# One-hots copied by ScalarE ahead of each gather's three products, in a graph network of two layers on one core

## The chip, the cores and the metric

The kernel runs on 1 core of one Trainium2 chip. The metric is device time in microseconds (us) of one execution, as the median of 10 executions. The core has five engines that run side by side and wait for each other by semaphores: TensorE (PE in the profile; its weight loads have a row of their own, PEld), VectorE (DVE), ScalarE (ACT), GpSimd (POOL) and SyncE (SP). An engine's instructions run in the order in which they stand in its queue.

## The reference

x is 12500 nodes of 256 features, and there are 200000 edges, sorted by target (dst). Cut to what matters:

```python
def _gcn_conv(x, W, b, src, dst, n):
    h = x @ W
    deg = jax.ops.segment_sum(ones, dst, num_segments=n)
    dinv = jnp.where(deg > 0, jax.lax.rsqrt(deg), 0.0)
    msgs = h[src] * (dinv[src] * dinv[dst])[:, None]
    return jax.ops.segment_sum(msgs, dst, num_segments=n) + b

def _L0(h):                       # edges plus one loop per node
    h = h @ W_pre + b_pre
    h = relu(_gcn_conv(h, W1, b1, src, dst, n))
    h = relu(_gcn_conv(h, W2, b2, src, dst, n))
    return h @ W_post + b_post

x = x + _L0(relu(layernorm(x)))
x = x + _L1(relu(layernorm(x)))   # attention over 4 heads of one edge per node
```

The weight is in the two convolutions: 200000 rows of a table are gathered by source, and summed by target.

## The kernel before

A first stage reads the edges, counts degrees, normalises x and writes a table of scaled rows to memory. Then `convolve` (L1155) runs twice, and a last stage does the attention layer.

**How a convolution is tiled.** The 200000 edges are cut into 112 chunks (`NCH`) of 14 gathers (`J`), a gather being 128 edges, whose source rows one indirect DMA fetches, one to a partition. The sorted targets of a chunk lie within a window of 128 nodes. So the sum by target is a matrix product: for each gather a one-hot matrix of 128 edges by 128 targets is the stationary operand (it has to be loaded as weights), and the gathered rows are the moving one, and all of the chunk is accumulated in one PSUM tile, `facc`.

**Three parts.** A float32 row is split into three bfloat16 rows whose sum it is (`to_parts`, L1475), and from chunk `SINCE` on in the first convolution, and throughout the second, the gather fetches the three side by side from the table `parts`. Then `many` is 3, and L1411 issues three products with the same one-hot and three different moving operands, into the same `facc`. Before `SINCE` the table is float32 and there is one product. Each product has its own load of weights in TensorE's queue.

**Buffers.** Nine gathers (`ONE`) share one `fgot` tile; the second convolution has four such tiles and the first five. GpSimd may run ahead of TensorE by what they hold, and then waits until TensorE is done with a tile. One VectorE instruction makes the one-hots of a whole chunk (`one_hots`, L1246, called by `hot_of` at L1410 when j is 2, for the chunk after), into `fhot`, which has three buffers of 14 one-hots each.

**Order of the work.** The loop at L1382 runs over the gathers (t counts them) and writes the instructions in the order wanted, with no scheduler behind it. For each gather: the indirect DMA on GpSimd (L1402); perhaps the one-hots of the next chunk; the products on TensorE (L1411); and then `run(t)`, which writes what is due at t. Due work is put down by `close` (L1290) at a chunk's end: ScalarE copies `facc` to `fsums` at once (L1293), 8 gathers later TensorE turns the sums (`turn_sums`, L1205), 13 later VectorE adds them into a sliding buffer, and where a tile of 128 nodes is then complete, `shift` (L1316) puts down the steps of `finish1` or `finish2`, each so many gathers later:

- `finish1` (L1446), first convolution: +6 TensorE's product with the folded weights (L1453) and the two-row product for the bias (L1454); +10 three ScalarE passes (L1458, L1460, L1462) and a DMA issued from ScalarE's queue (L1463); +12 VectorE's split into parts and SP's write of them (L1476 to L1479).
- `finish2` (L1542), second convolution: +6 TensorE (L1550); +8 VectorE and ScalarE (L1557, L1560); +12 TensorE (L1566); +14 VectorE, and a root on ScalarE (L1571 to L1579); +16 ScalarE (L1587); +26 TensorE (L1592); +28 ScalarE (L1596); +32 TensorE (L1605); +34 a ScalarE copy and two DMAs issued from its queue (L1613 to L1616).

There are 98 such tiles of nodes in 112 chunks. Every engine meets its instructions in the order in which the loop wrote them, so what ScalarE has to do for the steps stands between what it does for the gathers. L1663 is a tile that is never used and only keeps addresses apart. The last stage (from L1702) has, at L1749 and L1751, products that ScalarE copies out of PSUM by turns.

Of the kernel before, what the change touches and what calls it, by code (L numbers as in the profile page):

```python
# [8 lines left out]
F32 = mybir.dt.float32  # L9
BF16 = mybir.dt.bfloat16  # L10
I32 = mybir.dt.int32
AF = mybir.ActivationFunctionType
# [5 lines left out]
P = 128  # L18
# [395 lines left out]
def fast_path(  # L414
# [26 lines left out]
    nc = tc.nc  # L441
# [4 lines left out]
    J = 14  # L446
# [17 lines left out]
    nj = [min(J, -(-(E - c * CE) // P)) for c in range(NCH)]  # L464
# [115 lines left out]
    def raw_scaled(c):  # L580

        k = slice(c * J, (c + 1) * J)
        nc.vector.reciprocal(raw_sc[:, k], raw_sc[:, k])
        nc.vector.tensor_mul(raw_sc[:, k], raw_sc[:, k], d_src[:, k])
        nc.vector.scalar_tensor_tensor(raw_mv[:, k, 0], raw_mv[:, k, 0], -1.0, raw_sc[:, k],
                                       op0=ALU.mult, op1=ALU.mult)
        nc.vector.tensor_copy(raw[c][:, :, D], d_src[:, k])
        for j in range(J):
            v = raw[c][:, j, :D]
            i = c * J + j  # L590
            nc.scalar.activation(v, v, AF.Relu, bias=raw_mv[:, i, 0:1], scale=raw_sc[:, i:i + 1])
# [563 lines left out]
    def convolve(ep, table, stride, width, ahead, with_sum, psum, prepare, finish, parts, since,  # L1155
# [64 lines left out]
        def begin_sums():  # L1220
            for n0, rows in first_rows:
                v, n = {}, min(P, BW - n0)
                new_turned(v)
                turn_sums(rows, 0, v)
                nc.vector.tensor_copy(state["buf"][0][:, :, n0:n0 + n], v["pt"][:, :KC, :n])
                if with_sum:
                    nc.vector.tensor_copy(state["buf"][1][:, n0:n0 + n], v["ps"][:, 0, :n])
# [18 lines left out]
        def one_hots(h, to):  # L1246
            n = to.shape[1]
            nc.vector.tensor_tensor(h, iota_p[:, None, :].to_broadcast([P, n, P]),  # L1248
                                    to[:, :, None].to_broadcast([P, n, P]), ALU.is_equal)

        def new_hot(c):
            if since == 0:
                return ep.tile([P, J, P], BF16, name="fhot", bufs=3)
            h = ep.tile([P, J, P], F32, name="fhot", bufs=3)
            if c < since:
                return h
            h = h.rearrange("p j n -> p (j n)").bitcast(BF16)[:, :J * P]
            return h.rearrange("p (j n) -> p j n", n=P)

        def hot_of(c):  # L1260

            n = nj[c]
            h = new_hot(c)
            one_hots(h[:, :n, :], to_0 if lacking and c == 0 else to_t[:, c, :n])
            return h

        def new_rows_of():
            if with_sum:
                return new_got()
            return rows_p.tile([P, ONE, 3 * stride], BF16, name="fgot", bufs=ahead)  # L1270

        def late_sums():

            h = new_hot(0)
            one_hots(h, to_t[:, 0, :])
            froms = new_rows_of().rearrange("p j d -> p (j d)")[:, :J * D]
            froms = froms.rearrange("p (j d) -> p j d", d=D)
            assert stride == TW * P and D == TW * P
            for i in range(TW):
                one_hots(froms[:, :, i * P:(i + 1) * P], from_0[:, i, :])  # L1280
            px = psum.tile([P, KC, P], F32, name="fpt", bufs=1)
            for i in range(TW):
                for j in range(J):
                    nc.tensor.matmul(px[:, i, :], froms[:, j, i * P:(i + 1) * P], h[:, j, :],
                                     start=(j == 0), stop=(j == J - 1))
            many = work.tile([P, KC, P], F32, name="fz", bufs=2)
            nc.scalar.activation(many, px, AF.Copy)
            return many, [load_rows((NT - TW + i) * P, P) for i in range(TW)]
# [70 lines left out]
        hots = {0: hot_of(0)}  # L1359
        raw_lohi, raw_m = {}, {}  # L1360
        for c in range(1, len(raw)):
            raw_lohi[c] = raw_ends(c, rows_p.tile([P, 2 * CE], BF16, name="lohi_t",
                                                  bufs=len(raw) - 1))
# [4 lines left out]
        def raw_ahead(c, j):  # L1368
# [8 lines left out]
            elif j + 1 == J:  # L1377
                raw_sum(c, raw_m[c], fpt())()
                raw_scaled(c)

        assert KC == TW
        for t, (c, j) in enumerate(tiles):  # L1382
            if j == 0:
                acc = psum.tile([P, width], F32, name="facc", bufs=2 if not with_sum else 3)

            many = 1 if c < since else 3
            if many == 1:
                if j == 0:
                    gots = (raw + [spare])[c] if raw and c <= len(raw) else new_rows_of()
                got = gots[:, j, :]  # L1390
            else:
                i = (t - since * J) % ONE
                if i == 0:
                    gots = new_rows_of()
                    if since:
                        gots = gots.rearrange("p j d -> p (j d)").bitcast(BF16)
                        gots = gots[:, :ONE * 3 * stride].rearrange("p (j d) -> p j d", j=ONE)
                got = gots[:, i, :]
            some = lacking and c == 0
            if c >= len(raw):  # L1400
                rows_of = table if many == 1 else parts
                nc.gpsimd.indirect_dma_start(  # L1402
                    out=got, out_offset=None,
                    in_=rows_of[:(NT - TW) * P, :] if some else rows_of[:],
                    in_offset=bass.IndirectOffsetOnAxis(
                        ap=src_0[:, j:j + 1] if some else src_t[:, c, j:j + 1], axis=0))
            if j == 2 and some:
                late = late_sums()
            if j == (5 if some else 2) and c + 1 < NCH:
                hots[c + 1] = hot_of(c + 1)  # L1410
            for i in range(many):  # L1411
                nc.tensor.matmul(acc, hots[c][:, j, :], got[:, i * stride:i * stride + width],  # L1412
                                 start=(j == 0 and i == 0),
                                 stop=(j == nj[c] - 1 and i == many - 1 and not some))
            if some and j == nj[c] - 1:
                for i in range(TW):
                    nc.tensor.matmul(acc, late[0][:, i, :], late[1][i], start=False,
                                     stop=(i == TW - 1))
            if with_sum and t == J - 1:
                begin_sums()  # L1420
                ready(0)
            if j == nj[c] - 1:
                close(c, acc, t)
            if c + 1 < len(raw):
                raw_ahead(c + 1, j)
            if behind:
                behind(t)
            run(t)
# [230 lines left out]
    with tc.tile_pool(name="psum2", bufs=1, space=PSUM) as psum, \  # L1659
            tc.tile_pool(name="fwork2", bufs=2) as work, \  # L1660
            tc.tile_pool(name="edges2", bufs=1) as ep, \
            tc.tile_pool(name="fgots2", bufs=1) as rows_p:
        ep.tile([P, 3520], F32, name="apart")  # L1663
        loaded = {}

        def no_late_rows():
            none = work.tile([P, LW, H], F32, name="none", bufs=1)
            nc.vector.memset(none, 0.0)
            nc.sync.dma_start(table_e[(NT - LW) * P:, :].rearrange("(w p) h -> p w h", p=P),
                              none)  # L1670

        def load_sources():
            loaded["from"] = work.tile([P, CE], I32, name="to_all", bufs=1)
            nc.sync.dma_start(loaded["from"], src[:CE].partition_broadcast(P))

        def late_hots(i):
            nc.vector.tensor_scalar(hot_l[i], loaded["from"], float((NT - LW + i) * P), lane,
                                    op0=ALU.subtract, op1=ALU.is_equal)

        def load_targets(c):  # L1680
            loaded[c] = load_ends(work, c, 1)

        setup = [no_late_rows, load_sources]
        setup += [lambda i=i: late_hots(i) for i in range(LW)]
        for c in range(EARLY):
            setup += [lambda c=c: load_targets(c),
                      lambda c=c: turn_hots(ap, c, loaded[c], EARLY)]

        def set_up(t):
            i, r = divmod(t - 3 * J, J)  # L1690
            if r == 0 and 0 <= i < len(setup):
                setup[i]()

        convolve(ep, table2, D, D, 4, False, psum, lambda w: prepare2(work, w),
                 lambda w, b, s, pre, bias: finish2(work, psum, w, b, pre, bias), parts2, 0,
                 True, rows_p=rows_p, behind=set_up)

        for c in range(1, AC):
            own_rows(c)
# [150 lines left out]
```

## Time and profile before

| What | Value |
|---|---|
| median of 10 runs | 4154.22 us (4149.71 to 4157.21) |
| the profiled execution, its own time | 4152.55 us |
| its span, first instruction to last | 4150.8 us |
| PE busy | 2786.8 us (67%) |
| PEld busy | 1915.0 us (46%) |
| POOL busy | 3105.2 us (75%) |
| DVE busy | 1386.1 us (33%) |
| ACT busy | 622.1 us (15%) |
| mean granted TensorE clock | 0.731 |
| first convolution's three-part gathers issued | 564 to 2026 us |
| second convolution's gathers issued | 2032 to 3990 us |
| granted clock, 564 to 2030 us | 0.66 |
| granted clock, 2030 to 3990 us | 0.77 |

The profile is of one execution. A line of a group names the source line, the engine, the operation and the tiles (output, then inputs), then the number of instructions, a bar, the busy time in us and the mean length in ns of one, a bar, and the idle time of the engine just before these instructions with what ended it. A line of the timeline has the start and the length in us, and in square brackets the idle time before it. "issue" is idle time in which the engine waited for nothing that the profile shows. Matmuls overlap in the array, and their ends are modelled, so a row of one is longer than the time until the next can start. The granted clock is the share of full speed that TensorE is allowed at that time; here it is either 1.0 or 0.5, and a mean is a mix of the two.

### The profile page before, as it was taken

How to read it: one execution, taken by the hardware profiler on the slowest of the kernel's cores; microseconds unless marked ns; L12 is line 12 of the kernel's file. 1: busy time of each engine (PE TensorE's matmuls, PEld its weight loads, DVE VectorE, ACT ScalarE, POOL GpSimd, SP SyncE). 2: the span in 40 equal slices, each digit the busy share in tenths (PEclk: the TensorE clock that was granted, in tenths of full speed). 3: DMA queues.
4: the chain of work that ended last, by engine and by line, in shares of the span. 5: the costliest groups of instructions: out<-in, count | busy, mean ns of one | idle time of the engine just before them, and what ended most of it. 6: DMA issues, size and time to landing. Idle time of an engine off the chain costs nothing.

```text
span 4150.8 us, 38955 instructions
## 1 busy us (share of the span) xinstructions
PE 2786.8 (67%) x13306; PEld 1915.0 (46%) x13306; DVE 1386.1 (33%) x3009; ACT 622.1 (15%) x1625; POOL 3105.2 (75%) x3299
## 2 busy tenths in 40 slices
PE   7687767767767766667656666666666666666674
PEld 5465444434444444444444444444454444444452
DVE  7578532222222222222322222222222222222248
ACT  5433210100010000001001111111111111111122
POOL 7677777777777777777777777777777777777766
PEclk7688776666666666666678877777778777777776
DMA  8688766666666666666667777777677777676776
GB/s 270 188 236 245 220 177 183 187 183 181 185 185 181 182 187 183 182 182 187 185 181 202 187 179 180 181 183 181 180 180 185 179 180 182 180 180 180 184 194 199
DMA packets 413533, 787.28 MB, mean 190 GB/s; under 512 B 101005, under 2 KB 267172, under 8 KB 413324
## 3 DMA queue, kind: packets, MB, share of 16 engines
q0 software_dynamic: 197264, 594.53, 55.7%
q1 hardware_dynamic: 170214, 173.89, 13.2%
q10 hardware_dynamic: 45846, 16.27, 1.6%
q8 instruction: 107, 1.75, 0.2%
q14 instruction: 102, 0.84, 0.1%
HBM read 692.31 MB, written 92.05 MB: 189 GB/s over the span
## 4 chain that ended last, share of the span: by engine, by line
POOL 29%; issue 11%; DMA 8%; PE 2%; DVE 1%; ACT 0%; POOLq 0%; ACTq 0%; SPq 0%; DVEq 0%
POOL fgot L1402 28%; DMA fgot<-parts,fsrc_t 7%; POOL fal L1759 1%; PE facc L1412 1%; DMA fal<-table_l,fsrc_t 1%; PE fpz L1550 0%; PE fpo L1566 0%; PE fturn L1208 0%; PE fpx L1605 0%; DMA self<-ftable 0%; DVE fhot L1248 0%; DVE near L1782 0%; DMA fgot<-parts,src 0%; DVE far L1782 0%; PE fpt L1592 0%
## 5 line engine op out<-in xcount | busy, mean ns | idle before, releaser
L1402 POOL DMA_INDIRECT fgot<-parts,fsrc_t x2720 | 2574.7, 947 | 828.6 <-issue 796.9
L1412 PE MATMUL facc<-fgot,fhot 128*128 128x256 bf16 (+2 forms) x8986 | 1927.0, 356 | 1181.5 <-DMA fgot<-parts,fsrc_t 1101.3
L1412 PEld LDWEIGHTS <-fhot 128*128 128x128 bf16 x8202 | 980.3, 121 | 1749.0 <-issue 1484.1
L1248 DVE TENSOR_TENSOR fhot<-iota_p,to_t 128x1792 bf16<-128x1792 f32 (+1 forms) x224 | 449.1, 2005 | 0.0
L1402 POOL DMA_INDIRECT fgot<-ftable,fsrc_t x336 | 318.4, 948 | 118.2 <-issue 103.0
L1476 DVE TENSOR_TENSOR fpo<-fpo,fparts 128x256 f32<-128x256 f32 x97 | 41.8, 431 | 920.7 <-ACT fo L1462 920.7
L1557 DVE SCALAR_TENSOR_TENSOR fy<-rb,fb2c,fpz 128x128 f32<-128x128 f32 x194 | 58.8, 345 | 668.9 <-PE fpz L1550 667.9
L1310 DVE TENSOR_TENSOR buf<-buf,fturn 128x256 f32 x224 | 94.5, 422 | 422.8 <-PE fturn L1208 376.9
L1571 DVE SCALAR_TENSOR_TENSOR fx<-fpo,fdinv,fxb 128x256 f32<-128x256 f32 x97 | 46.9, 484 | 534.8 <-PE fpo L1566 534.8
L1412 PEld LDWEIGHTS facc<-fgot,fhot 128*128 128x128 f32 x784 | 165.9, 227 | 126.4 <-DMA fgot<-ftable,fsrc_t 74.5
L1293 ACT ACTIVATE fsums<-facc 128x257 f32<-128x257 f32 (+1 forms) x224 | 85.5, 382 | 874.2 <-PE facc L1412 867.4
L1453 PE MATMUL fpo<-wf,buf 128*128 128x256 f32 x388 | 162.0, 564 | 27.4 <-DVE buf L1310 27.3
L1550 PE MATMUL fpz<-buf,fwb 128*128 128x128 f32 x776 | 171.9, 396 | 1.0 <-DVE buf L1310 1.0
L1550 PEld LDWEIGHTS fpz<-buf,fwb 128*128 128x128 f32 x776 | 165.8, 314 | 6.9 <-DVE buf L1310 1.2
L1458 ACT ACTIVATE fpo<-fpo,fdinv 128x256 f32<-128x256 f32 x97 | 43.2, 445 | 573.4 <-PE fpo L1454 573.3
L1453 PEld LDWEIGHTS fpo<-wf,buf 128*128 128x128 f32 x388 | 105.0, 295 | 51.7 <-DVE buf L1310 32.4
L1208 PE MATMUL fturn<-fident,fsums 128*128 128x128 f32 x448 | 110.1, 337 | 3.6 <-ACT frow_p L1500 3.1
L1566 PE MATMUL fpo<-fwo,fz 128*128 128x256 f32 x388 | 110.1, 410 | 0.6 <-ACT fz L1560 0.6
L1208 PE MATMUL fturn<-fident,self 128*128 128x128 f32 x396 | 96.8, 335 | 19.6 <-DMA self<-ftable 13.6
L1596 ACT ACTIVATE ht<-fpt 128x256 f32<-128x256 f32 x97 | 37.2, 384 | 451.8 <-PE fpt L1592 450.8
L1560 ACT ACTIVATE fz<-fy 128x256 f32<-128x256 f32 x98 | 40.8, 417 | 404.7 <-DVE fy L1557 380.1
L1759 POOL DMA_INDIRECT fal<-table_l,fsrc_t x84 | 81.1, 966 | 25.6 <-issue 22.6
(284 smaller groups left out, 2417.2 us busy)
## 6 DMA issues: line engine op xcount, KB each, us to landing
fgot<-parts,fsrc_t POOLq DMA_INDIRECT x2720
parts<-frow_p SPq DMA_DIRECT2D x98, 195.0 KB
parts<-fparts SPq DMA_DIRECT2D x98, 192.0 KB
frow<-ftable SPq DMA_DIRECT2D x98, 130.0 KB
self<-ftable SPq DMA_DIRECT2D x99, 128.0 KB
self<-ftable SPq DMA_DIRECT2D x97, 130.0 KB
ftable<-fo ACTq DMA_DIRECT2D x98, 128.0 KB
kept_x<-fx SPq DMA_DIRECT2D x98, 128.0 KB
```

The costliest lines, as they stand in the source:

```text
L1208: nc.tensor.transpose(v["pt"][:, i * KC + k, :], rows[:, k * P:(k + 1) * P], ident)
L1248: nc.vector.tensor_tensor(h, iota_p[:, None, :].to_broadcast([P, n, P]), to[:, :, None].to_broadcast([P, n, P]), ALU.is_equal)
L1293: nc.scalar.activation(sb, acc, AF.Copy)
L1310: nc.vector.tensor_add(b, b, v["pt"][:, :KC, :])
L1402: nc.gpsimd.indirect_dma_start(out=got, out_offset=None, in_=rows_of[:(NT - TW) * P, :] if some else rows_of[:], in_offset=bass.IndirectOf ...
L1412: nc.tensor.matmul(acc, hots[c][:, j, :], got[:, i * stride:i * stride + width], start=(j == 0 and i == 0), stop=(j == nj[c] - 1 and i == ...
L1453: nc.tensor.matmul(po, buf[:, k, :P], wf[:, k, :], start=(k == 0), stop=False)
L1550: nc.tensor.matmul(pz[:, m, :], wb[:, k, m * P:(m + 1) * P], buf[:, k, :P], start=(k == 0), stop=(k == KC - 1))
L1557: nc.vector.scalar_tensor_tensor(y[:, m, :], v["root"], b2c[:, m:m + 1], v["pz"][:, m, :], op0=ALU.mult, op1=ALU.add)
L1566: nc.tensor.matmul(po, v["z"][:, m, :], wo[:, m, :], start=(m == 0), stop=(m == KC - 1))
L1571: nc.vector.scalar_tensor_tensor(x2, v["po"], dinv[:, w:w + 1], v["x"], op0=ALU.mult, op1=ALU.add)
L1759: nc.gpsimd.indirect_dma_start(out=al[:, i, :], out_offset=None, in_=(table_l if c else table_e)[:], in_offset=bass.IndirectOffsetOnAxis(a ...
```

## The change

Where a gather has three products, ScalarE first copies its one-hot, 128 by 128 in bfloat16, from the chunk's `fhot` into a tile `own_hot` with one buffer, and all three products take it from there. `AT_ONCE` says how many one-hots are copied by one instruction; it is 1. Chunks with one float32 product are as before. The padding tile in the second convolution is 64 columns smaller, which is what `own_hot` takes.

```diff
+        AT_ONCE = 1
+        assert J % AT_ONCE == 0
+
         assert KC == TW
         for t, (c, j) in enumerate(tiles):
...
             if j == (5 if some else 2) and c + 1 < NCH:
                 hots[c + 1] = hot_of(c + 1)
+            hot = hots[c][:, j, :]
+            if many > 1:
+                if j % AT_ONCE == 0:
+                    own = ep.tile([P, AT_ONCE, P], BF16, name="own_hot", bufs=1)
+                    n = min(AT_ONCE, nj[c] - j)
+                    nc.scalar.activation(own[:, :n, :], hots[c][:, j:j + n, :], AF.Copy)
+                hot = own[:, j % AT_ONCE, :]
             for i in range(many):
-                nc.tensor.matmul(acc, hots[c][:, j, :], got[:, i * stride:i * stride + width],
+                nc.tensor.matmul(acc, hot, got[:, i * stride:i * stride + width],
                                  start=(j == 0 and i == 0),
...
-        ep.tile([P, 3520], F32, name="apart")
+        ep.tile([P, 3456], F32, name="apart")
```

In the built program the first weight load of a gather waits for ScalarE's count, its first product waits for the gather's DMA, and the copy of a gather waits for TensorE's count after the last product of the gather before.

## The prediction

> **What bounds the kernel now.** I read the chain of waits first, then the costliest groups, then the timeline of each convolution.
>
> ```profile
> POOL 29%; issue 11%; DMA 8%; PE 2%; DVE 1%; ACT 0%; POOLq 0%; ACTq 0%; SPq 0%; DVEq 0%
> ...
> L1402 POOL DMA_INDIRECT fgot<-parts,fsrc_t x2720 | 2574.7, 947 | 828.6 <-issue 796.9
> L1412 PE MATMUL facc<-fgot,fhot 128*128 128x256 bf16 (+2 forms) x8986 | 1927.0, 356 | 1181.5 <-DMA fgot<-parts,fsrc_t 1101.3
> ```
>
> GpSimd issues a gather every 0.947 + 0.30 = 1.25 us and almost never waits for TensorE. TensorE waits 1101 us for gathers: it is the one with slack. A chunk of 14 gathers has 14 x 1.25 = 17.5 us. The program has 1171 three-part gathers in the first convolution (83.6 chunks) and 1563 in the second (111.6). So the question is whether TensorE and ScalarE, tied together by the change, still do a chunk in 17.5 us.
>
> The timeline shows the sizes, the first four lines from the second convolution, the next five from the first, the last two from the final stage:
>
> ```profile
> 2824.80 0.49 PE L1412 MATMUL facc<-fgot,fhot 128*128 128x256 bf16 x3 [0.75 <-DMA fgot<-parts,fsrc_t]
> 2825.32 0.38 ACT L1293 ACTIVATE fsums<-facc 128x256 f32<-128x256 f32 x1 [2.08 <-PE facc L1412]
> 2831.02 0.80 PE L1412 MATMUL facc<-fgot,fhot 128*128 128x256 bf16 x3 [0.37 <-DMA fgot<-parts,fsrc_t]
> 2831.61 1.91 PE L1550 MATMUL fpz<-buf,fwb 128*128 128x128 f32 x8
> ...
> 1430.10 1.91 PE L1453 MATMUL fpo<-wf,buf 128*128 128x256 f32 x4
> 1431.94 1.22 PE L1454 MATMUL fpo<-bb,fins 2*128 2x256 f32 x2
> 1433.09 2.12 PE L1412 MATMUL facc<-fgot,fhot 128*128 128x257 bf16 x9
> 1433.20 0.45 ACT L1458 ACTIVATE fpo<-fpo,fdinv 128x256 f32<-128x256 f32 x1 [8.70 <-PE fpo L1454]
> 1434.37 0.33 ACTq L1463 DMA_DIRECT2D ftable<-fo  x1
> ...
> 4034.10 0.39 ACT L1751 ACTIVATE fxg<-fends 128x260 f32<-128x260 f32 x1
> 4034.54 0.52 PEld L1749 LDWEIGHTS fends<-rows,hot_t 128*128 128x128 f32 x2 [0.34 <-ACT fxg L1751]
> ```
>
> A gather's three products take 0.49 us at full clock and 0.80 at half; ScalarE starts 0.04 us after their end, and a weight load 0.05 after a ScalarE end. Nine in a row in 2.12 us give 0.213 us of streaming each at half clock (0.107 at full), the rest is the last one's tail.
>
> Which clock is granted decides. These rows are two answers of the busy time by window (us, then busy time of TensorE, its weight loads, VectorE, ScalarE, GpSimd; then clock, DMA share, GB/s), cut where the clock can change:
>
> ```profile
> 1416.00:1419.41 3.41, 3.23 (x15) 2.31 (x14) 1.61 (x6) 0.00 (x0) 2.50 (x4) 0.50 0.60 165
> 1419.41:1422.83 3.42, 1.48 (x9) 0.86 (x9) 1.67 (x1) 0.00 (x0) 2.51 (x4) 1.00 0.59 166
> 1422.83:1426.24 3.41, 2.02 (x9) 1.11 (x9) 0.00 (x0) 0.39 (x1) 2.62 (x3) 0.50 0.62 165
> ...
> 2870.08:2873.49 3.41, 1.73 (x14) 1.30 (x13) 0.51 (x2) 0.42 (x1) 2.50 (x4) 1.00 0.86 139
> 2873.49:2876.91 3.42, 2.04 (x14) 1.60 (x14) 0.00 (x0) 0.38 (x1) 2.51 (x4) 1.00 0.71 233
> 2876.91:2880.32 3.41, 1.60 (x14) 1.10 (x12) 2.88 (x8) 1.66 (x4) 2.65 (x3) 1.00 0.65 177
> 2880.32:2883.73 3.41, 1.56 (x8) 1.07 (x8) 1.13 (x1) 0.13 (x1) 2.65 (x3) 0.50 0.83 247
> ```
>
> The first window streams 90% of its time and the next has full clock; the second streams nine products, 0.28, and half clock follows. Counted so over all windows from 600 to 3980 us (L1454's two-row and L1605's four-column products left out), full clock followed a half-clock window that streamed 0.745 or more, and half clock a full-clock window under 0.37; 98.5% obey.
>
> **The change part by part.** *Added: 2734 ScalarE copies of 128x128 bf16.* L1500's 128x260 copy takes 404 ns and L1332's 128x640 takes 736, 0.87 ns a column; 128 columns make 0.29 us. 2734 x 0.29 = 793 us, while ScalarE is busy 622 of 4151: as work alone it fits.
>
> *Added: two waits per gather.* The tile has one buffer, so the copy for gather j+1 waits for the last product of j, and the first weight load of j+1 waits for the copy. Before, that load ran ahead of the gather's landing. The round: copy 0.29; to the weight load 0.05; load to product, not shown for bf16, between 0 and the 0.21 by which loads lead products, taken as 0.12 at half clock and 0.08 at full; products 0.80 or 0.49; back 0.04; a separate event wait ahead of the copy, bounded by 0 and 0.10, taken as 0.04, the record of such an instruction. Sum 1.34 us at half clock (bounds 1.18 and 1.49), 0.99 at full (0.87 and 1.08). Neither is hidden once TensorE lags; between two gathers it now has a hole of 1.34 - 0.64 = 0.70 us (0.67 at full).
>
> *TensorE's other work* stands in program order between gathers and fills the hole. What exceeds it, at half clock:
> - first convolution: turning sums, 6 x 0.213 = 1.28, exceeds by 0.6; L1453 and L1454, from 1430.10 to 1433.09 = 2.99, by 2.3.
> - second: turning 0.86, by 0.15; L1605, 0.1; L1550, 1.71, by 1.0; L1566 with L1592, 2.14, by 1.45.
>
> *ScalarE's other work* is queued in order with the copies. fsums (L1293) stands between the last copy of a chunk and the first of the next: 0.3 of its 0.38. L1458 to L1463, 1433.20 to 1434.70 = 1.5, exceeds by 0.45 the 1.05 in which ScalarE is free in a round. fz, h, ht and fxa with its two DMA issues (1.0 us) lie inside that. Behind a waiting copy stand these evictions; VectorE's split, TensorE's next step and SP's row writes wait for them, all several gathers early. *Moved:* the fhot buffer is released by ScalarE instead of TensorE, one chunk ahead of need: nothing. The smaller padding tile costs nothing; it issues no instruction.
>
> The L1453 group ran in 60 of 69 chunks (0.87). At half clock, first convolution: 14 x 1.34 + 0.3 + 0.6 + 0.87 x 2.75 = 22.1 us a chunk; second: 18.8 + 0.3 + 0.15 + 0.87 x 2.55 = 21.5. At full clock, the same sums with halved streaming: 16.2 and 14.7.
>
> *How much at which clock.* Gathers alone stream 0.64/1.34 = 0.48 at half clock, too little to raise it, and 0.32/0.99 = 0.32 at full, too little to keep it. Denser places raise it. First convolution: turning between two gathers makes 0.64 + 1.28 + 0.64 = 2.56 us without a hole, which meets 0.745 of a window in 63% of the window's positions; L1453 in 18%. One window of 3.4 us at full clock follows, a little more after L1453: 3 of 14 gathers. Second: L1550 makes 2.99 us (76%), and then turning and L1566 keep the clock to the chunk's end, 8.5 gathers; else L1566 alone brings 3.5. Together 0.87 x 7.2 + 0.1 = 6.4 of 14. Each such gather saves 0.35, and L1566 at full clock 0.7 a chunk on average. Chunks: 22.1 - 1.05 = 21.0 and 21.5 - 2.2 - 0.7 = 18.6.
>
> Sum: 83.6 x 3.5 = +293, 111.6 x 1.1 = +123, in all +416. The profiled execution took 4152.55 us (span 4150.8), 1.7 under the median of 4154.22; 4153 + 416 = 4569, say 4570. The ring of four nine-gather tiles lets GpSimd run 45 us ahead and then wait for facc; that cover is spent once.
>
> [...]
>
> **The rivals.**
> - *The cover holds: no change, 4154.* At full clock both chunks (16.2, 14.7) are under 17.5. It decides if the round at full clock is 0.87 us or less, since 0.32/0.87 = 0.37 keeps the clock by itself; that is my lower bound. For it: 1101 us of slack. Against: every uncertain term would have to be at its least. Chance 0.07.
> - *Half clock throughout.* If the dense places don't raise the clock, 83.6 x 4.6 + 111.6 x 4.0 = +831: 4985. For it: bursts of several gathers, which raise it now (x9 at 1433.09), are gone. Against: L1550 at 1.71 us stays. Chance 0.14.
> - *Only the first convolution lags:* the second's chunks stay under 17.5, and +293 alone gives 4445. Chance 0.18.
> - *The copy is free of the wait*, were the buffer doubled by the planner: in the built order every copy but a chunk's first waits for TensorE's count, so no. A gain would need GpSimd to issue faster, which nothing here touches.
>
> **How the numbers follow.** Forecast 4570, chance 0.58; the range 4300 to 4900 takes in the third rival, and the bounds of the round (0.15 x 14 x 195 = 410 either way, partly offset by the clock). Left out: no change, half clock throughout, and 0.03 for what I have not thought of. Faster by over 0.2% (about what a measurement tells from no change) 0.02; within 0.07; slower 0.91.
>
> **What would show it.** After: GpSimd's waits for facc in hundreds of us where there were 15; TensorE's idle time put down to own_hot's copy, not to the gathers; copies of 0.29 us, 0.08 to 0.12 us after the products; a gather each 1.0 or 1.34 us where none of the steps stands; a first-convolution chunk near 21 us, a second near 18.6. Wrong if the copy takes over 0.35 us, if full clock lasts through gathers alone, or if TensorE still waits for landings.

## The result, and the profile after

| | before | after |
|---|---|---|
| median | 4153.9 us (28 runs) | 4378.17 us (8 runs, 4360.69 to 4385.4) |
| ratio | | 1.0533, interval 1.0523 to 1.0543 |
| profiled execution, span | 4150.8 us | 4365.3 us |
| first convolution's three-part gathers, to the second's first | 563.9 to 2032.5 us | 564.1 to 2237.7 us |
| second convolution's gathers | 2032.5 to 3989.4 us | 2237.7 to 4194.7 us |

The change costs 5.3%, 224 us. The range holds it; the forecast of 4570 was 192 too high. The loss lies almost wholly in the first convolution, 205 us of the span's 214.5. The second takes the same 1957 us as before, and the last stage starts 8 us later behind its end.

The page's chain of waits, which led the reading of before, breaks off in the last stage of after (its shares add up to some 5%):

```profile
POOL 1%; DVE 1%; DMA 1%; issue 1%; PE 1%; ACT 0%; ACTq 0%; DVEq 0%; POOLq 0%
```

So I read the costliest groups of after instead (number of instructions, busy us, mean ns of one, idle us just before and what ended it):

```profile
L1405 POOL DMA_INDIRECT fgot<-parts,fsrc_t x2720 | 2574.3, 946 | 973.8 <-issue 762.5
L1422 PE MATMUL facc<-fgot,own_hot 128*128 128x256 bf16 (+1 forms) x8202 | 1887.7, 356 | 1107.7 <-ACT own_hot L1419 1030.3
L1419 ACT ACTIVATE own_hot<-fhot 128x128 bf16<-128x128 bf16 x2734 | 841.9, 308 | 2285.2 <-PE facc L1422 2250.9
```

L1405 is the gather (L1402 before), L1422 the products, L1419 the new copy. TensorE still has 1108 us of idle time before its products (1182 before), but now 1030 of it is put down to the copy, where 1101 was put down to landing gathers. It is no longer slack: where no other work of TensorE stands between two gathers, each idle stretch has the same length, and it comes in every round, so a gather that comes late stays late. GpSimd, which sets the pace, has 145 us more of idle time. The view of waits names it (us in all, times, longest), first before, then after:

```profile
POOL fgot L1402 <- PE facc L1412: 15.0, 22, 8.4
```

```profile
POOL fgot L1405 <- PE facc L1422: 201.8, 159, 9.7
POOL fgot L1405 <- DVE self L1201: 65.4, 1, 65.4
```

The wait for `facc` grew from 15.0 to 201.8 us. In the first convolution GpSimd's gaps beyond the usual 0.3 us add up to 145 us, the first of 3 us at 941 us: from there on GpSimd has run ahead as far as the tiles allow and moves at TensorE's pace. The last line is one wait, GpSimd's first gather of the second convolution, which was 5.1 us long: it is the time TensorE needs for the gathers still ahead of it. 145 and 60 make the 205.

TensorE's timeline of after in the first convolution shows the round (start, length, idle time before):

```profile
1402.07 0.51 PE L1422 MATMUL facc<-fgot,own_hot 128*128 128x257 bf16 x3 [0.46 <-ACT own_hot L1419]
1403.04 0.51 PE L1422 MATMUL facc<-fgot,own_hot 128*128 128x257 bf16 x3 [0.46 <-ACT own_hot L1419]
...
1406.79 0.83 PE L1422 MATMUL facc<-fgot,own_hot 128*128 128x257 bf16 x3 [0.46 <-ACT own_hot L1419]
1408.08 0.83 PE L1422 MATMUL facc<-fgot,own_hot 128*128 128x257 bf16 x3 [0.46 <-ACT own_hot L1419]
1409.37 0.83 PE L1422 MATMUL facc<-fgot,own_hot 128*128 128x257 bf16 x3 [0.46 <-ACT own_hot L1419]
1409.99 1.91 PE L1463 MATMUL fpo<-wf,buf 128*128 128x256 f32 x4
1411.83 1.22 PE L1464 MATMUL fpo<-bb,fins 2*128 2x256 f32 x2
1412.98 0.83 PE L1422 MATMUL facc<-fgot,own_hot 128*128 128x257 bf16 x3
```

Where only gathers follow each other, the hole is always 0.46 us: a gather each 0.97 us at full clock and 1.29 at half. GpSimd's pace is 1.25. At half clock the round alone is slower than a gather's issue, and L1463 with L1464 then makes one interval of 3.61 us (1409.37 to 1412.98).

The windows of both convolutions (length, then busy us of TensorE, its weight loads, VectorE, ScalarE, GpSimd; then granted clock, DMA share, GB/s), first before, then after:

```profile
560.00:2030.00 1470.00, 1031.19 (x4437) 625.54 (x4438) 360.90 (x697) 134.58 (x343) 1109.91 (x1174) 0.66 0.67 183
2030.00:4050.00 2020.00, 1303.27 (x7097) 967.61 (x7095) 560.62 (x1181) 256.32 (x679) 1520.31 (x1605) 0.77 0.71 184
```

```profile
560.00:2030.00 1470.00, 1026.66 (x3914) 463.32 (x3913) 318.78 (x611) 419.31 (x1333) 1014.16 (x1075) 0.58 0.61 166
2030.00:4050.00 2020.00, 1390.87 (x6867) 811.88 (x6867) 529.79 (x1103) 669.03 (x2199) 1466.86 (x1549) 0.73 0.68 176
```

In the first convolution the clock falls from 0.66 to 0.58 though TensorE is as busy as before: its busy time comes from fewer instructions (3914 instead of 4437) that each last longer.

### The profile page after: what moved, and what is told of

Same layout as the page of the kernel before. It is cut to its first block, busy times and chain, and to the rows that moved or that the text cites. A ratio compares the mean times of both kernels' runs of the same rounds, so it can differ in the third digit from the quotient of the medians.

```text
span 4365.3 us, 44043 instructions
## 1 busy us (share of the span) xinstructions
PE 3011.1 (69%) x13306; PEld 1686.3 (39%) x13306; DVE 1385.9 (32%) x3009; ACT 1390.2 (32%) x4359; POOL 3107.3 (71%) x3299
## 5 line engine op out<-in xcount | busy, mean ns | idle before, releaser
L1405 POOL DMA_INDIRECT fgot<-parts,fsrc_t x2720 | 2574.3, 946 | 973.8 <-issue 762.5
L1422 PE MATMUL facc<-fgot,own_hot 128*128 128x256 bf16 (+1 forms) x8202 | 1887.7, 356 | 1107.7 <-ACT own_hot L1419 1030.3
L1422 PEld LDWEIGHTS <-own_hot 128*128 128x128 bf16 x8202 | 727.5, 114 | 2181.9 <-ACT own_hot L1419 1932.5
L1419 ACT ACTIVATE own_hot<-fhot 128x128 bf16<-128x128 bf16 x2734 | 841.9, 308 | 2285.2 <-PE facc L1422 2250.9
L1248 DVE TENSOR_TENSOR fhot<-iota_p,to_t 128x1792 bf16<-128x1792 f32 (+1 forms) x224 | 449.0, 2005 | 0.0
L1405 POOL DMA_INDIRECT fgot<-ftable,fsrc_t x336 | 318.0, 946 | 119.5 <-issue 103.8
L1422 PE MATMUL facc<-fgot,fhot 128*128 128x257 f32 x784 | 244.8, 457 | 61.3 <-DMA fgot<-ftable,fsrc_t 47.6
L1422 PEld LDWEIGHTS facc<-fgot,fhot 128*128 128x128 f32 x784 | 161.5, 223 | 132.7 <-DMA fgot<-ftable,fsrc_t 82.3
L1463 PE MATMUL fpo<-wf,buf 128*128 128x256 f32 x388 | 168.7, 584 | 23.7 <-DVE buf L1310 23.7
L1463 PEld LDWEIGHTS fpo<-wf,buf 128*128 128x128 f32 x388 | 109.9, 309 | 49.1 <-DVE buf L1310 28.2
L1464 PE MATMUL fpo<-bb,fins 2*128 2x256 f32 x194 | 100.8, 613 | 0.0
```

Source lines behind the costliest of these rows:

```text
L1405: nc.gpsimd.indirect_dma_start(out=got, out_offset=None, in_=rows_of[:(NT - TW) * P, :] if some else rows_of[:], in_offset=bass.IndirectOf ...
L1419: nc.scalar.activation(own[:, :n, :], hots[c][:, j:j + n, :], AF.Copy)
L1422: nc.tensor.matmul(acc, hot, got[:, i * stride:i * stride + width], start=(j == 0 and i == 0), stop=(j == nj[c] - 1 and i == many - 1 and ...
L1463: nc.tensor.matmul(po, buf[:, k, :P], wf[:, k, :], start=(k == 0), stop=False)
L1464: nc.tensor.matmul(po, fs, bb, start=False, stop=True)
```

## The experiments

The theory (A): the single tile makes a chain of copy and products of fixed length for each gather; the hole in it also keeps the clock at half; where the chunk at that clock is longer than GpSimd's 17.5 us, the time is lost, and nowhere else. Against it stood the copies as mere work, the waits without the clock, and the layout. Diffs are against the kernel after unless said; where a small tile is added, the padding tile is 64 columns smaller again. A ratio is to the kernel before, run beside it.

**Two tiles.** The smallest edit that takes the chain away and leaves the copies.

```diff
-                    own = ep.tile([P, AT_ONCE, P], BF16, name="own_hot", bufs=1)
+                    own = ep.tile([P, AT_ONCE, P], BF16, name="own_hot", bufs=2)
```

> own_hot has two buffers, so the copy of a gather can run while the products of the gather before still read the other tile; the number of copies stays 2734. Theory A (the closed round of one tile costs the time): the round opens, TensorE keeps up with a gather each 1.25 us again, and the time is 4154 +- 10. Theory B (ScalarE's added work, or its order in the queue, costs the time): 4378 stays, at most 20 us less.

4164.98 us, ratio 1.0033 (1.0021 to 1.0044). What remains is 13.5 us over the kernel before beside it, so some 211 of the 224 us are gone; A said at most 10 us would remain.

**Copies made, not read.** The line that makes the products take the copy is left out, so the products read `fhot` and ScalarE still makes all 2734 copies.

```diff
-                hot = own[:, j % AT_ONCE, :]
```

> All 2734 copies are made, but the products take their one-hots from fhot as before the change, so no copy waits for TensorE and no load for ScalarE. Theory A (the round): 4154 +- 10. Theory B (some 840 us of copies on ScalarE delay the evictions that others wait for): over 4250.

4162.18 us, ratio 1.0028 (1.0017 to 1.0040). 842 us of copies on ScalarE come with 11 us more, so the copies as work are not it.

**Two one-hots at a time.** A round for two gathers has the hole once instead of twice.

```diff
-        AT_ONCE = 1
+        AT_ONCE = 2
```

> One copy of 256 columns for two gathers, one buffer. The round takes 0.31 + 0.11 for the copy, and six products: 2.03 us at half clock for two gathers, 1.39 at full. Theory A: at full clock it streams 0.64 of 1.39 = 0.46, over the 0.37 that keeps the clock, and even at half clock a gather takes 1.02 us: TensorE keeps up, 4154 to 4170. Rival (each wait between the engines costs by itself, half as many waits cost half): 4265.

4166.38 us, ratio 1.0032 (1.0019 to 1.0045). Still one buffer, still a wait in each round, but one that is paid once for two gathers: A holds.

**The change in one convolution only.**

```diff
-            if many > 1:
+            if many > 1 and with_sum:          # first
+            if many > 1 and not with_sum:      # second, in a run of its own
```

> The copies are made in the first convolution alone. From the trace of after, where the first convolution is 205 us longer and the second issues its gathers in the same 1957 us: theory A (all of it comes from the first convolution): 4150 + 205 = 4355 to 4365. Rival (the second gives back or loses something that its own backlog hides): 4300 or less.

> The copies are made in the second convolution alone. Theory A (its chunk is at 17.4 us just under the 17.5 that GpSimd takes): 4154 to 4175, the rest being the backlog of 5 to 11 gathers that is worked off at the end. Rival (in after, the second convolution is helped by a late start or otherwise): over 4200.

First only: 4369.83 us, ratio 1.0523 (1.0505 to 1.0540), 5 us past the range that was expected. Second only: 4182.8 us, ratio 1.0091 (1.0062 to 1.0120), 31 us above before, 8 past the range that was expected. The trace of the second shows GpSimd's gathers issued at the old times, 2031.2 to 3987.6 us, with 13 to 28 gathers issued that TensorE has not begun (3 to 7 in before). The price falls due only at the end, where GpSimd's first gather of the last stage waits for the last rows. The wait in before, in the second alone, and in the whole change:

```profile
POOL fal L1759 <- ACT fxl L1613: 8.9, 1, 8.9
```

```profile
POOL fal L1769 <- DMA table_l<-fxl: 36.6, 1, 36.6
```

```profile
POOL fal L1769 <- ACT fxl L1623: 17.0, 1, 17.0
```

So 28 of the 31 us are this one wait. The two runs together lose 218 + 31, more than the 224 of the whole change: in the whole, GpSimd starts the second convolution late, right behind TensorE, and is only 4 to 14 gathers ahead, so its last wait is 17.0 us.

**The hole filled with zero products.** To tell the clock from the waits: two products with an all-zero one-hot of 256 columns follow each gather's three, in the hole. They add zeros to the sums.

```diff
+            if many > 1:
+                for i in range(2):
+                    nc.tensor.matmul(acc, zero, got[:, :width], start=False,
+                                     stop=(j == nj[c] - 1 and i == 1 and not some))
```

> After a gather's three products stand two more with an all-zero one-hot of their own tile; they add zeros to facc, and the copy of the next gather doesn't wait for them. They lie in the hole of the round (0.65 us at half clock against 2 x 0.213). Theory A (the round is too slow only because its holes leave TensorE at half clock): streaming rises from 0.50 to 0.83 of the time at half clock and from 0.33 to 0.55 at full, the clock stays at full in both convolutions, a round takes 0.97 us, and more work makes the kernel faster: 4154 to 4175. Rival (the clock follows, but isn't the cause; more TensorE work is more time): 4378 or more, up to 5 products of 0.213 and a hole of 0.46 each gather, 4600.

4169.74 us, ratio 1.0041 (1.0027 to 1.0055): TensorE has 5468 products more to do, and the kernel is 208 us faster than after. Its windows, as above:

```profile
560.00:2030.00 1470.00, 1067.17 (x6751) 639.87 (x6752) 359.69 (x694) 473.79 (x1507) 1109.86 (x1174) 0.93 0.66 183
2030.00:4050.00 2020.00, 1505.46 (x10195) 1038.90 (x10194) 546.05 (x1156) 682.52 (x2234) 1506.55 (x1589) 0.93 0.69 182
```

The clock goes from 0.58 to 0.93, and in the first convolution GpSimd issues its 1174 instructions in 1470 us again, as before. The chain of copy and products is still there, with a round of 0.97 us in the median; it just runs at the clock at which it is short enough.

**The same products in the kernel before.** If the clock alone were worth something, before would gain from it as well.

> The kernel before, with the two zero products after each gather's three, no copies. It raises the clock to near 0.9 as in the changed kernel. Theory (before is paced by GpSimd's 1.25 us a gather, whatever the clock): no gain, 4152 to 4165, of which up to 10 from the shifted addresses. Rival (before loses time to the half clock as well): 4130 or less.

4164.57 us, ratio 1.0026 (1.0017 to 1.0035), with a mean clock of 0.867 where before has 0.731. Nothing gained: GpSimd sets the pace of before at either of these clocks. Of these two runs the faster clock paid only where TensorE was late (208 us less than after).

**A longer round.** A second copy into an unused half of the tile is put ahead of each real one.

```diff
-                    own = ep.tile([P, AT_ONCE, P], BF16, name="own_hot", bufs=1)
+                    own = ep.tile([P, AT_ONCE + 1, P], BF16, name="own_hot", bufs=1)
                     n = min(AT_ONCE, nj[c] - j)
+                    k = min(j, nj[c] - 2)
+                    nc.scalar.activation(own[:, 1:, :], hots[c][:, k + 1:k + 2, :], AF.Copy)
```

> A second copy of 128 columns into a spare half of own_hot precedes each copy, in the same round: 0.31 less the 0.09 by which two ScalarE instructions overlap, 0.22 us a gather, so rounds of 1.50 and 1.18 us. Theory A: the first convolution's chunk becomes some 22.6 us (+5.1 over GpSimd's 17.5, 83.6 chunks: +427), the second's, which stood just under the bound, some 20 (+279): 4860, between 4750 and 4950. Rival (the second convolution has room, its gathers are paced by GpSimd): only the first lags, 4580.

4996.78 us, ratio 1.2029 (1.2000 to 1.2058), 47 us past the upper end of what was expected. Its timeline:

```profile
1402.97 0.83 PE L1424 MATMUL facc<-fgot,own_hot 128*128 128x257 bf16 x3
1404.46 0.83 PE L1424 MATMUL facc<-fgot,own_hot 128*128 128x257 bf16 x3 [0.66 <-ACT own_hot L1421]
1405.95 0.83 PE L1424 MATMUL facc<-fgot,own_hot 128*128 128x257 bf16 x3 [0.66 <-ACT own_hot L1421]
```

0.20 us more in each of 2734 rounds would be 547 us; 619 came on top of after. The rest goes with a lower clock, 0.53 and 0.64 in the two stretches of the windows above instead of 0.58 and 0.73. And now the second convolution is late too, from 2505 to 4785 us: its chunks are just under GpSimd's pace in after, so little of what is added is hidden.

**The copies on VectorE.** Its copy is shorter, 0.228 us in the mean in this run where ScalarE's takes 0.308 in after; a round under some 0.87 us should keep full clock, by the prediction's estimate.

```diff
-                    nc.scalar.activation(own[:, :n, :], hots[c][:, j:j + n, :], AF.Copy)
+                    nc.vector.tensor_copy(own[:, :n, :], hots[c][:, j:j + n, :])
```

> VectorE makes the same copies instead of ScalarE, one buffer. The smallest VectorE copies in the trace of before take 0.15 to 0.21 us, so the round shrinks by 0.10 to 0.16 from 0.97 and 1.29, to some 0.84 and 1.16 us. Theory A with its threshold (0.32 of streaming over the round reaches 0.37 when the round is 0.87 us): full clock now keeps itself through gathers alone, the first convolution's clock rises from 0.58 to over 0.7, and TensorE keeps up: 4155 to 4185. Rival (the time goes in proportion to the round, the clock's share staying): 14 x 0.13 = 1.8 of the 2.4 us a chunk that the first convolution lost: 4228. VectorE's 2 us one-hots once a chunk stand in its queue before a copy and can add up to 1.5 us a chunk in both.

4437.62 us, ratio 1.0679 (1.0657 to 1.0701): worse than after, and past both expectations. The granted clock from 560 to 2030 us is 0.59, where over 0.7 was expected. VectorE's timeline says why:

```profile
1435.92 0.27 DVE L1419 COPY own_hot<-fhot 128x128 bf16<-128x128 bf16 x1 [0.92 <-PE facc L1422]
1436.11 2.01 DVE L1248 TENSOR_TENSOR fhot<-iota_p,to_t 128x1792 bf16<-128x1792 f32 x1
1438.04 0.18 DVE L1419 COPY own_hot<-fhot 128x128 bf16<-128x128 bf16 x1
```

The round alone is shorter, 0.79 us at full clock and 1.12 at half. But where L1248, the one-hots of the next chunk, stands between two copies, they start 2.04 us apart in the median instead of 1.12; with VectorE's sums it is 2.09, with the split into parts 1.37. In the first convolution that takes about what the shorter rounds gain (the second begins at 2241 us, 2238 in after); the second, which loses nothing in after, issues its gathers in 2011 us instead of 1957. With the rounds broken up like this, the time says nothing of the clock's edge. It shows that here a short instruction that is needed every 1.25 us does badly in a queue with long ones (L1248's 2.01 us).

**The clock's edge.** One zero product of 32 or of 128 columns after the three of each gather but a chunk's last.

```diff
+            if many > 1 and j < nj[c] - 1:
+                nc.tensor.matmul(acc[:, :ZC], zero, got[:, :ZC], start=False, stop=False)
```

> The changed kernel with one zero product of 32 columns after a gather's three (not after a chunk's last gather), in the hole of the round. At full clock the round of 0.97 us streams 0.32 + 0.01 = 0.34 of its time, still under the 0.37 that keeps the clock. Theory A: full clock still ends within gathers alone; 4330 to 4380. Rival (any product more is time more, or the clock has no such edge between 32 and 128 columns): the same time as e12_zero_128.

> The same with 128 columns: 0.32 + 0.05 of 0.97 = 0.385 at full clock, over the 0.37. At half clock 0.64 + 0.11 of 1.29 = 0.58, not enough to raise the clock, so the turning of the sums still has to raise it once, but then it stays until TensorE has caught up. Theory A: 4160 to 4200, and the clock of the first convolution rises from 0.58 to over 0.64. Rival: no edge, 4330 to 4380 as with 32 columns.

32 columns: 4425.41 us, ratio 1.0634 (1.0616 to 1.0652). 128: 4378.4 us, ratio 1.0526 (1.0509 to 1.0544). Both expectations were too low, and the time with 128 columns lies where the rival without an edge put it; against that rival speaks only that 32 columns took 47 us more. Rounds without a step in them stay at 0.967 and 1.288 us, but the zero product stands ahead of TensorE's steps and lengthens the interval with L1463's products from 3.61 to 3.83 us, for which 32 columns bring nothing in return. With 32 columns the second convolution begins at 2273 us, 36 later than in after, of which that interval, 75 times, is some 16; the wait at the end is 42.3 us, 25 more than in after. The rest was not taken apart. At 128 columns the clock rises only a little (windows of that run):

```profile
560.00:2030.00 1470.00, 1105.71 (x4844) 587.49 (x4842) 314.76 (x601) 415.26 (x1323) 1010.66 (x1068) 0.60 0.60 165
2030.00:4050.00 2020.00, 1454.74 (x8329) 947.96 (x8328) 531.47 (x1108) 670.32 (x2201) 1470.26 (x1549) 0.77 0.67 177
```

I had worked out 0.37 us of streaming in a round of 0.97, 0.385, just over the 0.37 counted in before. So I counted the traces again as for the prediction, by windows of 3.41 us: each of the 520 stretches of one clock in the trace of before, and of the 406 in that of after, is a whole number of these long, but for the last, with which the record ends. "Kept" is the share of full-clock windows with nothing but gathers in them that full clock followed:

| kernel | edge that separates best: to keep full clock / to raise half | windows of gathers alone at full clock: number, median streaming (first, second convolution) | kept (first, second) |
|---|---|---|---|
| before | 0.37 / 0.745 | | |
| after | 0.375 / 0.74 | 55, 88: 0.31, 0.29 | 0, 0 |
| 32 zero columns | 0.38 / 0.76 | 58, 86: 0.34, 0.30 | 0.14, 0 |
| 128 zero columns | 0.38 / 0.78 | 78, 101: 0.35, 0.33 | 0.26, 0.06 |
| two of 256 | | 205, 116: 0.48, 0.45 | 0.81, 0.68 |

In these traces the edge is about where it was in before; some 1 to 4% of the windows disobey it. It was my 0.385 that was wrong: by this count, which cuts 0.165 us off the end of each modelled product (an estimate of its tail, from 0.80 - 3 x 0.213 and 0.49 - 3 x 0.107 us in before), gathers with 128 zero columns stream 0.33 to 0.35, and stay under it. The two-row and four-column products are left out of this count: counted like others, they raise the windows of before that disobey its edges from 7 to 79 of 989. The zero products count like others (left out of the count, 6.6% of the full-clock windows of that run disobey the best edge, with them 4.3%). No run was made with a size between 128 and 512 columns, so the edge is read from traces and not tried from both sides by itself.

**Addresses alone.** Every version without the loss stayed 10 to 17 us above before. The kernel before with an unused tile of `own_hot`'s size, and not an instruction more:

```diff
+        ep.tile([P, P], BF16, name="pad_hot", bufs=1)
         for t, (c, j) in enumerate(tiles):
...
-        ep.tile([P, 3520], F32, name="apart")
+        ep.tile([P, 3456], F32, name="apart")
```

> The kernel before, with an unused tile of 128 bf16 columns where own_hot stands, and the smaller padding tile: no instruction more, only addresses as in the change. The kernels with an opened round are still 10 to 13 us over before, and their traces show it where the convolutions meet: GpSimd's first gather of the second waits 13 to 18 us, 5.1 before, for a VectorE fill of another tile. Theory (the shifted addresses of the first convolution make the second's first fgot tile share memory with work that ends later): 4158 to 4163 here too. Rival (the copies' own work does it): 4152 +- 2.

4162.12 us, ratio 1.0021 (1.0011 to 1.0030). At the crossing into the second convolution GpSimd waits for another buffer, and longer. The waits of before, then of this run:

```profile
POOL fgot L1402 <- DVE fins L1447: 5.1, 1, 5.1
```

```profile
POOL fgot L1403 <- DVE self L1201: 14.7, 1, 14.7
```

That is 9.6 us more, where the medians differ by 8.2: it accounts for all of it. With two tiles this wait is 18.1 us, with the copies unread 14.6. No version ran faster than before; as GpSimd's issue bounds it, I would expect that of none of this kind.

## Why the prediction was right or wrong

**The mechanism** was right: TensorE and ScalarE as a chain of fixed length, the clock held down by the hole in it (0.58 in the first convolution, 0.93 with the hole filled), GpSimd waiting for `facc`. Two tiles, two at a time and the filled hole each take it away. But the sum was not: +416 us where +224 came. Of the forms it could take, the third rival came about (only the first convolution lags; its price of 4445 was still 67 too high), and not the forecast. That the result lies in the range is owed to the range having been drawn wide enough for that rival. The rival "the cover holds" fell with the first convolution. "Half clock throughout" is refuted by the share of copies made at full clock, 0.21 to 0.23 in the first convolution (by where in the copy it is counted) and 0.57 to 0.58 in the second. The copy was not free of the wait.

**The clock** went as the prediction's count of before had it. Where only gathers follow each other, the holes in after are 0.46 us, and of its 143 full-clock windows of gathers alone (55 and 88, with a median streaming of 0.31 and 0.29, under the 0.37) none was followed by full clock. The edges that separate best are 0.37 and 0.745 in the trace of before, 0.375 and 0.74 in that of after.

**Two terms were mis-sized: the round at half clock**, 1.34 us forecast, 1.287 measured, **and the share of the second convolution's gathers at full clock**, 6.4 of 14 forecast, 8.1 measured. The steps of the round, as medians over the copies:

| step | forecast | measured |
|---|---|---|
| copy | 0.29 | 0.309 |
| to the weight load | 0.05 | 0.050 |
| load to product | 0.12 (bounds 0 and 0.21) | 0.004 |
| three products | 0.80 | 0.83 |
| product's end to the copy | 0.04 + 0.04 | 0.097 |

The product started 0.004 us after its weight load, so the lower bound of 0 was nearly the value. With the copy and the other steps 0.053 remains, but a chunk has 14 rounds. The forecast lay 1.1 us a chunk above GpSimd's 17.5 in the second convolution. The shorter round alone takes off some 0.6 of it (0.75 less at half clock, but each gather at full clock then saves 0.32 instead of 0.35), and the larger share at full clock some 0.5: it took both to turn +123 us into nothing.

The two chunks, with the terms as measured except two of the second that are taken as forecast:

| term, us a chunk | first: forecast | first: measured | second: forecast | second: measured |
|---|---|---|---|---|
| 14 rounds at half clock | 18.8 | 18.0 | 18.8 | 18.0 |
| `fsums` at the border | 0.3 | 0.22 | 0.3 | 0.22 |
| turning and ScalarE's steps | 0.6 + 0.4 | 0.58 | in 2.4 | taken as 2.4 |
| L1463, L1464 | 2.0 | 2.0 | | |
| gathers at full clock | 3.0 x 0.35 = -1.05 | 3.0 x 0.32 = -0.96 | 6.4 x 0.35 = -2.24 | 8.1 x 0.32 = -2.58 |
| L1566 at full clock | | | -0.7 | taken as -0.7 |
| chunk | 21.0 | 19.9 | 18.6 | 17.4 |

- *First convolution.* 205 / 83.6 = 2.45 us a chunk over 17.5 is a chunk of 19.95, which is what the terms give; 84 intervals between two `fsums` have a mean of 19.7. Beside the round, turning and ScalarE's L1468 to L1473 were added up (0.6 and 0.4) though they fall into the same interval and overlap; together they cost 0.58. The price of L1463 and L1464 (2.3 forecast, 3.61 - 1.287 = 2.32 measured) and the share at full clock (3 of 14 forecast, 0.21 to 0.23 measured) were right. Copies near 0.29 us (0.309) and waits put down to own_hot came as expected. The sum for this chunk at full clock, 16.2, does not follow from the prediction's terms: halved like the second's, they make some 15.3 to 15.8. Both are under 17.5, and nothing else rests on it.
- *Second convolution.* Full clock lasts longer than forecast, 0.576 of the copies, counted at their start, against 6.4 of 14 = 0.457. No run shows why; that a shorter round streams a larger share of its time (0.64 of 1.287 us is 0.50, forecast 0.48) may be part of it. With the round that makes 17.4, a hair under 17.5, though with two terms of the forecast still in it. Measured directly, 108 intervals between two `fsums` have a mean of 17.46 us; they run from 15.7 to 20.5, and the lead of GpSimd takes up the difference.
- *Not in the sum:* the end, 8 us, and the address shift, some 8 to 10 us, which lies inside the 65 us wait at the crossing. The padding tile was costed at nothing because it issues no instruction. It has an effect without one (8 us in the run with addresses alone).

The sums close: 416 forecast; 88 less in the first convolution, 123 less in the second, 8 more at the end make 213, and the profiled span grew by 214.5.

## What to carry to other kernels

A copy through a single buffer between two engines added a round trip to every iteration here, and the test is whether the round with that hole in it, at the lower clock, is still shorter than the pace of the engine that bounds; a second buffer or two items per round took all but some 13 us of the loss away. Idle time "with slack" is no cover if it is one stretch in every round, and here holes in TensorE's stream cost a second time through the clock (0.58 in the first convolution, 0.66 before). Where a forecast chunk lies within a few per cent of the bound, the chance belongs on both sides of it: 0.05 us in a round and 1.7 gathers more at full clock in a chunk decided 123 us here.

## What the runs showed of the hardware that I had not expected

- Two products with all-zero weights after each gather's three took the granted clock of the first convolution from 0.58 to 0.93, with 5468 products more and 208 us less.
- A tile that is never used changed the time by 8 us, through the buffer that GpSimd's first gather of the second convolution then waits for (14.7 us where it was 5.1).
- Filling the hole by a little (32 columns) was worse than leaving it (ratio 1.0634 where after has 1.0533); part of it is that what is put into the hole also stands ahead of the work that does not fit into it (3.83 us where it was 3.61).
